# Projections of a conditioned attention layer: block products of 128 output rows, or four products of 32 output rows side by side

## The chip, the cores and the metric

The kernel runs on one core of a Trainium2 chip. The metric is the device time of one execution in microseconds (us), the median of three runs. A core has five engines with a queue of instructions each: TensorE (PE in the profile; its weight loads are listed apart as PEld), VectorE (DVE), ScalarE (ACT), GpSimd (POOL) and SyncE (SP), which here issues nearly all transfers. A matmul of TensorE holds one operand (the stationary one) in the array and streams the other (the moving one) through it; its sums go to PSUM, which has eight banks of 128 partitions x 512 f32.

## The reference

Eight batches of 512 tokens with 512 features go through one attention layer with 16 heads of 32 features; a conditioning token per batch is projected too and added to the queries and keys, and the input is added to the output.

```python
def _L0_cond_ref(x, tokens, Wq, bq, Wk, bk, Wv, bv):
    Q = _split_heads(x @ Wq.T + bq)
    K = _split_heads(x @ Wk.T + bk)
    V = _split_heads(x @ Wv.T + bv)
    tQ = _split_heads(tokens @ Wq.T + bq)
    tK = _split_heads(tokens @ Wk.T + bk)
    cQ = Q + tQ
    cK = K + tK
    scores = jnp.einsum('bhqd,bhkd->bhqk', cQ, cK) / jnp.sqrt(jnp.float32(HEAD_DIM))
    attn = jax.nn.softmax(scores, axis=-1)
    out = jnp.einsum('bhqk,bhkd->bhqd', attn, V)
    ...
x = x + _L0_cond_ref(x, cond_1024[:, None, :], ...)
```

## The kernel before

**Tiling.** Everything is f32 except small bf16 helpers. A *tile of work* t is four heads (128 features) of one batch: T = 8 x 4 = 32 of them, t = 4b + g. Queries and keys stand with features on partitions (`qT`, `kT`, 128 x 512 for one t), values with tokens on partitions (`v`).

**Projections.** The projections Q, K and V are made in 2 x 2 blocks with seven block products in place of eight (`MADE_OF` lists which sum of weight blocks meets which sum of input blocks; `combine_w` and `combine_x` make the sums `wc` and `xc` ahead of time). For one projection n, one batch b and one half u of the output, `product` (L397) makes block product i: a contraction over 256 features in two chunks kc, so two f32 matmuls of a 128 x 128 stationary operand with a 128 x 256 moving one, into half a bank. For q and k the weights are stationary and the input moves (L406); for v the input is stationary and the weights move (L403). `first_products` (L431) makes products 1, 6, half of 2, and 7, with a copy by ACT (`m1`, L438) and three additions by DVE (L444, L445, L429 or L426). `other_products` (L448) makes 4, 5, the other half of 2, and 3, then three wider additions by DVE (L458, L459, L429 or L426). Either one issues seven matmuls. In both, a call `small()` stands in the middle: after product 6, or after product 5.

**Stages.** The order on PE, ACT, DVE and POOL is written out by hand (`manual_schedule`): instructions run on each engine in the order of the code. The main loop (L796, t = 0 to 28) has four stages for each t. Each stage begins with `exponentials` of one 128-token chunk of keys: four matmuls with `onesb` and `maxT` (L560, three rows, bf16) and four with `kT` and `qT` (L563, 32 rows) into four banks, which ACT then takes the exponential of (`e`, L574). Then comes `row_max` of a later chunk: four score matmuls of 32 rows (L499) into the other four banks, from which DVE takes negative row maxima (L490 twice, L508) and after that ACT exponentials with a running sum (`dead`, L518, in `denominators`). Then the stage's own part follows:

- first stage: half of the q products of a later batch (`project_pair`),
- second stage: `weighted` (L617), that is values times `e` in 128 x 32 column tiles (`times_v`, L579), the denominators spread the same way (L610), a transpose by DVE (L635) and the stores,
- third stage: half of the k products,
- fourth stage: half of the v products, with `transpose_max` (L539) as its `small()`: four bf16 128 x 128 transposes on PE (L544) and a copy by DVE (L550) that makes the `maxT` of the next t.

A row of products is made in two stages, `first_products` in one t and `other_products` in the next, so the two alternate. The q and k products in the loop belong to t = 1 to 28, the v products with transposes to t = 0 to 28. Four stages of products stand ahead of the loop (L749 to L761), three of v without transposes in its t = 0 (L806, L822, L832). The last tiles (from L904) have no products.

**PSUM.** All eight banks are one tile; `TURNS` says for each stage which bank is used for what. So a score matmul L499 waits until the bank that it writes has been read: by ACT (`dead` of the stage before) or by DVE (the last addition of the products of the stage before).

**Shapes on TensorE.** Three ways to divide the array occur: 32 rows x 128 columns (L560, L563, L499: four heads side by side on different rows), 128 rows x 32 columns (L579, L610: four outputs side by side on different columns), and the whole 128 x 128 (L403, L406, L544). Every f32 matmul of the code appears in the trace as two weight loads and two matmuls.

Of the kernel before, what the change touches and what calls it, by code (L numbers as in the profile page):

```python
# [17 lines left out]
def kernel(  # L18
# [38 lines left out]
    nc = tc.nc  # L57
    P = 128
    B, S, D = x.shape
    HD = 32  # L60
    H = D // HD
    G = D // P
    HG = P // HD
# [5 lines left out]
    HS = S // 2  # L69
# [175 lines left out]
    for i in range(NS):  # L245
        r = slice(i * BL, (i + 1) * BL)
# [130 lines left out]
    def block_of_w(n, i, u, kc):  # L377
        f = MADE_OF[i - 1][0]
        if n == "v":
            at = slice(0, HS) if f != "22" else slice(HS, D)  # L380
            if isinstance(f, int):
                return wc[n][:, f, kc, :]
        else:
            g = u * 2 + (f == "22")
            at = slice(g * P, (g + 1) * P)
            if isinstance(f, int):
                return wc[n][:, f, kc, u * P : (u + 1) * P]
        return wT[n][:, kc + 2 * (f != "11"), at]

    def block_of_x(b, i, kc, at):  # L390
        f = MADE_OF[i - 1][1]
        if isinstance(f, int):
            return xc[:, f, kc, at]
        off = HS * (f == "22")
        return xT[b][:, kc + 2 * (f != "11"), at.start + off : at.stop + off]

    def product(n, b, u, i, pt, kcs=(0, 1)):  # L397

        for kc in kcs:
            w = block_of_w(n, i, u, kc)  # L400
            if n == "v":
                xb = block_of_x(b, i, kc, slice(u * P, (u + 1) * P))
                nc.tensor.matmul(pt, xb, w, start=(kc == kcs[0]), stop=(kc == kcs[-1]))  # L403
            else:
                xb = block_of_x(b, i, kc, slice(0, HS))
                nc.tensor.matmul(pt, w, xb, start=(kc == kcs[0]), stop=(kc == kcs[-1]))  # L406

    def twice(a):
        return a.unsqueeze(1).broadcast_to([P, 2, HS])
# [21 lines left out]
    def first_products(n, b, u, dens, small, at, first=0):  # L431


        one_, two_ = banks(first), banks(at)
        c1, c12, c2, c22 = parts_of(n, b, u)
        m1 = c2[:, 0, :]
        product(n, b, u, 1, one_[:, :HS])
        nc.scalar.copy(m1, one_[:, :HS])  # L438
        dens()
        product(n, b, u, 6, two_[:, :HS])  # L440
        small()
        product(n, b, u, 2, two_[:, HS:], (0,))
        product(n, b, u, 7, one_[:, HS:])
        nc.vector.tensor_tensor(c12, two_[:, :HS], m1, ALU.add)  # L444
        nc.vector.tensor_tensor(c1[:, 0, :], two_[:, HS:], m1, ALU.add)  # L445
        plus(n, b, u, 1, c22, one_[:, HS:], c12)
# [349 lines left out]
    for t in range(T - 3):  # L796
        b, r = divmod(t, G)
# [201 lines left out]
    b, g = divmod(t, G)  # L999
# [55 lines left out]
```

## Time and profile before

| what | value |
|---|---|
| median of 3 runs (lowest, highest) | 729.93 us (729.53, 730.05) |
| span of the profiled execution, first to last instruction | 727.7 us |
| granted TensorE clock, mean | 1.000 |
| PE busy | 720.6 us (99%), 5412 matmuls |
| PEld busy | 406.0 us (56%), 5412 loads |
| ACT busy | 616.6 us (85%) |
| DVE busy | 536.5 us (74%) |
| POOL busy | 175.9 us (24%) |
| block products of v, L403 | 448 matmul records |
| block products of q and k, L406 | 840 matmul records |

The profiled execution has no time of its own beside its span; the span is 2.2 us below the median of the runs, the part that lies around the first and the last instruction. A group line of the profile gives engine, line, operation, the tiles written and read, and the shape: for a matmul, rows*columns of the stationary operand and then the moving operand. A matmul's record starts when it enters the array; its end is modelled, so records of matmuls that follow each other overlap, and the distance from start to start is what counts. Two numbers at the head of a timeline line are the start in us from the beginning of the span and how long the merged records last; x4 is the number of records; a bracket is idle time of the engine before them and what ended it.

### The profile page before, as it was taken

The numbers are of one execution on the slowest core, as the hardware profiler recorded it, in microseconds if no ns is written. First come the engines' busy times: TensorE is split into PE (matmuls) and PEld (weight loads), VectorE is DVE, ScalarE is ACT, GpSimd is POOL, SyncE is SP. The second block draws the span as 40 slices with busy tenths as digits, with TensorE's granted clock in tenths as the row PEclk, the third lists the DMA queues.
The fourth block names the chain that finished last, engine by engine and source line by source line (L and its number), as shares of the span: only waits on it lengthen the run. The fifth ranks groups of instructions, "written<-read, shape, count | busy, mean of one in ns | idle before, by whom it ended". The sixth has DMA issues, their size and how long they took to land.

```text
span 727.7 us, 15109 instructions
## 1 busy us (share of the span) xinstructions
PE 720.6 (99%) x5412; PEld 406.0 (56%) x5412; DVE 536.5 (74%) x863; ACT 616.6 (85%) x1539; POOL 175.9 (24%) x275
## 2 busy tenths in 40 slices
PE   9999999999999999999999999999999999999997
PEld 7566555566555566555566555565555565555532
DVE  4798777777768777678776877777767777767777
ACT  2589898899898898888899888888988989888664
POOL 3711221122221122221122221122221122221351
PEclk9999999999999999999999999999999999999999
DMA  6743221222221222221222221212110111110111
GB/s 176 110 64 49 45 45 23 38 39 36 44 44 21 40 34 40 45 41 23 42 33 41 44 40 22 44 31 43 31 23 9 31 29 31 30 20 11 30 31 29
DMA packets 207583, 29.12 MB, mean 40 GB/s; under 512 B 205834, under 2 KB 206346, under 8 KB 207508
## 3 DMA queue, kind: packets, MB, share of 16 engines
q1 hardware_dynamic: 205748, 27.11, 22.5%
q10 hardware_dynamic: 1760, 1.05, 0.5%
q8 instruction: 42, 0.69, 0.4%
q14 instruction: 33, 0.27, 0.1%
HBM read 19.75 MB, written 8.39 MB: 39 GB/s over the span
## 4 chain that ended last, share of the span: by engine, by line
PE 96%; DVE 2%; DMA 1%; issue 1%; DVEq 0%; SPq 0%
PE psum L406 27%; PE psum L499 16%; PE psum L579 15%; PE psum L403 14%; PE psum L563 14%; PE psum L560 5%; PE psum L350 2%; PE psum L544 1%; DVE acc L855 1%; DMA x<-in_x_dram 1%; PE psum L881 1%; PE psum L657 0%; DVE acc L853 0%; PE psum L589 0%; PE psum L266 0%
## 5 line engine op out<-in xcount | busy, mean ns | idle before, releaser
L518 ACT ACTIVATE dead<-psum,nmax 128x512 f32<-128x512 f32 x480 | 327.0, 701 | 5.2 <-DVE nmax L490 3.1
L574 ACT ACTIVATE e<-psum 128x512 f32<-128x512 f32 x488 | 251.9, 603 | 71.5 <-PE psum L563 71.2
L490 DVE TENSOR_REDUCE nmax<-psum 128x1 f32<-128x512 f32 x240 | 154.5, 685 | 142.8 <-PE psum L499 142.8
L508 DVE TENSOR_REDUCE nmax<-psum 128x2 f32<-128x1024 f32 x130 | 157.6, 1214 | 2.7 <-PE psum L499 2.7
L499 PE MATMUL psum<-kT,qT 32*128 32x512 f32 x1024 | 142.6, 601 | 0.0
L636 POOL TENSOR_TENSOR res<-res,recs 128x512 f32<-128x512 f32 x30 | 31.4, 1047 | 439.0 <-DVE res L635 439.0
L563 PE MATMUL psum<-qT,kT 32*128 32x512 f32 x976 | 125.5, 587 | 0.0
L579 PE MATMUL psum<-e,v 128*32 128x512 f32 x1024 | 121.2, 597 | 0.0
L518 ACT ACTIVATION_READ_ACCUMULATOR dead<-psum,nmax 128x1 f32 x480 | 104.8, 218 | 0.0
L499 PEld LDWEIGHTS psum<-kT,qT 32*128 32x128 f32 x1024 | 59.7, 183 | 57.1 <-ACT dead L518 19.6
L579 PEld LDWEIGHTS psum<-e,v 128*32 128x32 f32 x1024 | 26.6, 110 | 65.1 <-issue 37.6
L563 PEld LDWEIGHTS psum<-qT,kT 32*128 32x128 f32 x976 | 48.6, 185 | 2.2
L403 PE MATMUL psum<-wc_v,xc 128*128 128x256 f32 x192 | 49.3, 379 | 0.0
L560 PE MATMUL psum<-maxT,onesb 3*128 3x512 bf16 x488 | 48.2, 385 | 0.0
L406 PE MATMUL psum<-xc,wc_k 128*128 128x256 f32 x180 | 46.2, 379 | 0.0
L406 PE MATMUL psum<-xc,wc_q 128*128 128x256 f32 x180 | 46.2, 379 | 0.0
L560 PEld LDWEIGHTS <-onesb 3*128 3x128 bf16 x488 | 12.3, 91 | 57.2 <-issue 47.9
L173 POOL TENSOR_TENSOR xr<-xr,bvs 128x512 f32<-128x512 f32 x31 | 39.3, 1268 | 17.4 <-DMA xr<-in_x_dram 17.4
L403 PEld LDWEIGHTS psum<-wc_v,xc 128*128 128x128 f32 x192 | 36.5, 190 | 4.9
L403 PE MATMUL psum<-wT_v,xT 128*128 128x256 f32 x128 | 38.8, 405 | 0.0
L637 POOL TENSOR_TENSOR res<-res,xr 128x512 f32<-128x512 f32 x30 | 38.2, 1273 | 2.3
L406 PEld LDWEIGHTS psum<-xc,wc_q 128*128 128x128 f32 x180 | 34.2, 190 | 4.6
(165 smaller groups left out, 819.5 us busy)
## 6 DMA issues: line engine op xcount, KB each, us to landing
xr<-in_x_dram SPq DMA_DIRECT2D x124, 64.0 KB, 2.4
out_dram<-res SPq DMA_DIRECT2D x122, 64.0 KB, 1.9
x<-in_x_dram SPq DMA_DIRECT2D x112, 64.0 KB, 2.3
w_q<-in_L_cond_Wq_dram SPq DMA_DIRECT2D x4, 256.0 KB, 4.5
w_v<-in_L_cond_Wv_dram SPq DMA_DIRECT2D x16, 64.0 KB, 2.4
w_k<-in_L_cond_Wk_dram SPq DMA_DIRECT2D x16, 48.0 KB, 2.6
x<-in_x_dram ACTq DMA_DIRECT2D x2, 256.0 KB, 3.9
x<-in_x_dram SPq DMA_DIRECT2D x2, 256.0 KB, 4.1
```

Source lines behind the costliest of these rows:

```text
L173: nc.gpsimd.tensor_tensor(xr[t], xr[t], bias, ALU.add)
L403: nc.tensor.matmul(pt, xb, w, start=(kc == kcs[0]), stop=(kc == kcs[-1]))
L406: nc.tensor.matmul(pt, w, xb, start=(kc == kcs[0]), stop=(kc == kcs[-1]))
L490: nc.vector.tensor_reduce(nmax[t][:, qc, j : j + 1, 0], banks(HG + j), AX.X, ALU.max, negate=True)
L499: nc.tensor.matmul(pt, qkT["q", t][r, qc * P : (qc + 1) * P], qkT["k", t][r, :], start=True, stop=True,)
L508: nc.vector.tensor_reduce(nmax[t][:, qc, pr * 2 : pr * 2 + 2, 0], pt, AX.X, ALU.max, negate=True)
L518: nc.scalar.activation(dead, banks(HG + j), AF.Exp, bias=nmax[t][:, qc, j, :], accum_out=sums[t][:, qc, j, :],)
L560: nc.tensor.matmul(bank[j], onesb[r, :], maxT[t][r, :], start=True, stop=False)
L563: nc.tensor.matmul(bank[j], qkT["k", t][r, kc * P : (kc + 1) * P], qkT["q", t][r, :], start=False, stop=True,)
L574: nc.scalar.activation(e[:, i, :], bank[pr * 2 + i], AF.Exp)
L579: nc.tensor.matmul(pt[j * HD : (j + 1) * HD, :], vs[b % 2][:, kc, (g * HG + j) * HD : (g * HG + j + 1) * HD], es[t, kc, j // 2][:, j % 2, ...
L637: nc.gpsimd.tensor_tensor(y, y, xr.pop(t), ALU.add)
```

## The change

Each matmul of a block product (128 columns of the stationary operand) is written as four matmuls with 32 columns each. Matmul j takes columns 32j to 32j+31 of the stationary operand, streams the same moving operand, and writes partitions 32j to 32j+31 of the output. `start` and `stop` are as before. `HG` is 4 and `HD` is 32. Nothing else of the kernel is changed; `times_v` and `spread_sums` are written in this way already.

```diff
         for kc in kcs:
             w = block_of_w(n, i, u, kc)
             if n == "v":
-                xb = block_of_x(b, i, kc, slice(u * P, (u + 1) * P))
-                nc.tensor.matmul(pt, xb, w, start=(kc == kcs[0]), stop=(kc == kcs[-1]))
+                still, moving = block_of_x(b, i, kc, slice(u * P, (u + 1) * P)), w
             else:
-                xb = block_of_x(b, i, kc, slice(0, HS))
-                nc.tensor.matmul(pt, w, xb, start=(kc == kcs[0]), stop=(kc == kcs[-1]))
+                still, moving = w, block_of_x(b, i, kc, slice(0, HS))
+            for j in range(HG):
+                r = slice(j * HD, (j + 1) * HD)
+                nc.tensor.matmul(
+                    pt[r], still[:, r], moving, start=(kc == kcs[0]), stop=(kc == kcs[-1])
+                )
```

## The prediction, made before the changed kernel ran

> **What bounds the kernel now.** I read the page first (busy time, then the chain that ended last), then TensorE's timeline over some stages, then the timelines of weight loads, VectorE and ScalarE around the stages' borders.
>
> ```profile
> span 727.7 us, 15109 instructions
> ...
> PE 96%; DVE 2%; DMA 1%; issue 1%; DVEq 0%; SPq 0%
> ```
>
> The end is set by PE almost alone. The timeline shows what it pays. First two whole stages (weighted, then one of v), then a place in the tail where four transposes stand between two 128x32 groups:
>
> ```profile
> 313.33 0.40 PE L560 MATMUL psum<-maxT,onesb 3*128 3x512 bf16 x4
> ...
> 314.42 1.02 PE L499 MATMUL psum<-kT,qT 32*128 32x512 f32 x8
> 315.37 1.07 PE L579 MATMUL psum<-e,v 128*32 128x512 f32 x8
> ...
> 316.31 2.76 PE L579 MATMUL psum<-e,v 128*32 128x512 f32 x24
> 319.01 0.40 PE L560 MATMUL psum<-maxT,onesb 3*128 3x512 bf16 x4
> ...
> 325.38 1.11 PE L499 MATMUL psum<-kT,qT 32*128 32x512 f32 x8
> 326.42 1.13 PE L403 MATMUL psum<-wT_v,xc 128*128 128x256 f32 x4
> 327.39 1.03 PE L403 MATMUL psum<-wc_v,xc 128*128 128x256 f32 x4
> 328.25 0.39 PE L544 MATMUL psum<-identb,split 128*128 128x128 bf16 x4
> 328.48 0.65 PE L403 MATMUL psum<-wT_v,xT 128*128 128x256 f32 x2
> 328.96 1.03 PE L403 MATMUL psum<-wc_v,xT 128*128 128x256 f32 x4
> 329.92 0.40 PE L560 MATMUL psum<-maxT,onesb 3*128 3x512 bf16 x4
> ...
> 692.53 1.07 PE L579 MATMUL psum<-e,v 128*32 128x512 f32 x8
> 693.53 0.40 PE L544 MATMUL psum<-identb,split 128*128 128x128 bf16 x4
> 693.86 1.07 PE L579 MATMUL psum<-e,v 128*32 128x512 f32 x8
> ```
>
> Two things are to be seen. The distance from start to start inside one shape is constant: (1.03 - 0.38)/3 = 0.216 us for a 256-column record of L403, (2.76 - 0.59 - 0.02)/5 = 0.429 us for a group of four column tiles of L579, whose four records start 7 ns apart. And every change of shape leaves a hole: the last record of L499 starts at 314.42 + 1.02 - 0.59 = 314.85, streams 0.43, and the next shape starts only at 315.37, 0.09 later; 0.52 from start to start in either stage.
>
> **The streaming.** An f32 matmul of a product is two records of 0.216 us. After the change it is two groups of four records. A group of L579 streams 512 columns in the time that one 128x128 record would take for them (0.429 is twice 0.216 less a few ns), so a group with 256 columns takes 0.216 us as well: 644 product matmuls, 1288 records before, 1288 groups after, difference nothing. No row shows four column tiles reading one moving operand; I allow 1 ns a group either way, 1.3 us.
>
> **Issue.** PE's instructions for a product stage go from 28 to 112 in 14 x 0.216 = 3.02 us, 27 ns each. The trace bounds this from both sides. The highest rate that it holds over microseconds is the weighted stage: 40 loads and 40 matmuls (L579 and 8 of L610) from 315.37 to 319.01, 46 ns each; were that the most that TensorE is fed, a stage would last 112 x 46 = 5.15 us, +2.1, and 92 stages +196 us. In a burst right after a wait the eight loads at 325.32 (below) start within 0.34 - 0.18 = 0.16 us with seven matmuls between them, 15 instructions at 11 ns. The weighted stage is paced by its streams (0.429 a group), not by its feed, so the burst is the nearer row, and I cost issue at nothing; the streaming hides it.
>
> **Weight loads.** The record of a load falls from 190 ns (128 columns) to 110 (32 columns). Loads hide beneath the matmul before them, so only the first after a hole shows: the first L403 group lasts 1.13 where an unhindered one lasts 1.03, so 0.104 us (483 against 379 ns for its first record). The first record of L579 lasts 617 against a median of 592 ns, so 0.025 us. Each product stage gains 0.079 us on entry. What if the cover is gone and every group shows its load: 1288 x 0.025 = 32 us. L579's loads start 2 ns after the matmul before and leave its 0.429 unchanged, so I take nothing.
>
> The Trainium skill (TensorE: Matmul & The Clock Gate, "What overlaps and what doesn't") speaks against the change here: it says that a weight load runs beside a matmul only if the two use different row groups, and column tiles all use the same rows. With its load time (columns / 1.2 ns, so 27 ns) that would be an estimated 1288 x 27 ns = 35 us. The same page ("Wait — 56ns, not 53.3ns?") gives 62 ns of sequencer time for a matmul when hardware decoding is off; 56 matmuls a stage would be 3.5 us for 3.02, an estimate of up to 41 us over 92 stages. The start of L579's loads contradicts the one, the burst the other.
>
> **Leaving a product stage.** Before: last record of L403 at 328.96 + 1.03 - 0.38 = 329.61, L560 at 329.92, 0.31. From column tiles: last L579 record at 316.31 + 2.76 - 0.59 = 318.48, L560 at 319.01, 0.53, less 0.213 for the shorter stream, 0.31 again; but the last tile starts 0.02 after the first. Cost 0.020 us a stage. Entry and exit together: -0.059 us.
>
> **The transposes in the v stages** are where a cost is added. Before, L544 has the same shape as L403 and no hole. Afterwards it stands between column tiles, and the tail shows just this. There, from the last tile of the group ahead (692.53 + 1.07 - 0.59 = 693.01) to the last tile of the second group behind (694.34) is 1.33 us; two streams of 256 columns fewer give 1.33 - 2 x 0.213 = 0.90. Before, 328.04 to 328.75 is 0.71. Cost 0.19 us, two holes in place of none. So a v stage with transposes pays -0.059 + 0.188 = +0.129 us.
>
> **PE alone** would give: 92 product stages, of them 29 of v with transposes (+0.129), 62 plain (-0.059), and one ahead of the loop that has its transposes in front (148 against 55 ns to the first product, 241 against 273 ns to the second group, 20 ns on leaving: +0.081). Sum 3.74 - 3.66 + 0.08 = +0.16 us.
>
> **But the gains of q and k meet another wait.** What is next late is the bank for the scores L499 in the stage behind:
>
> ```profile
> 321.15 1.29 DVE L490 TENSOR_REDUCE nmax<-psum 128x1 f32<-128x512 f32 x2 [1.20 <-PE psum L499]
> 324.45 0.75 DVE L429 SCALAR_TENSOR_TENSOR kT<-psum,tok,kT 128x512 f32<-128x512 f32 x1
> ...
> 298.45 2.06 ACT L574 ACTIVATE e<-psum 128x512 f32<-128x512 f32 x4 [0.95 <-PE psum L563]
> 303.21 0.24 ACT L518 ACTIVATION_READ_ACCUMULATOR dead<-psum,nmax 128x1 f32 x1
> ...
> 325.32 0.34 PEld L499 LDWEIGHTS psum<-kT,qT 32*128 32x128 f32 x8 [0.60 <-ACT dead L518]
> 303.51 0.30 PEld L499 LDWEIGHTS psum<-kT,qT 32*128 32x128 f32 x6 [0.23 <-ACT dead L518]
> ```
>
> Behind `other_products`, VectorE runs without a pause from L490 (freed by the scores of the same stage) through L508, L458, L459 to L429, which ends at 325.20; the loads of L499 start at 325.32, and its group lasts 1.11 where an unhindered one lasts 1.02: 0.09 us lost. Behind `first_products`, ScalarE runs without a pause from `e` (freed by L563) over the copy and four `dead` to 303.45; the load comes at 303.51 and the scores lose 0.09 again. Both chains begin ahead of the products, so neither moves when the products end 0.059 sooner: L499 ends when it did. The q `other` kind, 0 to 14 ns from its wait in the trace (load 314.30, exposed 0.10, matmul 314.42), has nothing to give either. So the 56 loop stages of q and k give nothing, bounds -3.3 us (all of it, if no chain held) and +1 us (20 ns a stage if loads bunch). In the v stages no such cover helps: the scores of the q stage behind them (L499 at 309.15, lasting 1.02) wait for nothing, so the cost is whole.
>
> **Sum.** 29 x 0.129 = +3.74 us; four stages ahead of the loop, 3 x -0.059 + 0.081 = -0.10; three v stages of t = 0, two of them held, -0.06 at most; the edge of q, 14 x -0.003 = -0.04. Total +3.6 us: span 727.7 to 731.3, and with the 2.2 us between span and median, 729.93 to **733.5 us** (0.5% slower).
>
> **Rivals.**
>
> *A, the gains are kept* (VectorE and ScalarE are let go earlier too): then PE's own sum, +0.16 us, 730.1. For it: 96% of the chain is PE. Against: the two waits above. 13%.
>
> *B, loads or issue show.* In column tiles of 256 columns the load has half the cover that it has in L579. If each group shows 25 ns, 32 us: 762. It decides once a load takes over 0.216 us in all; its record is 110 ns. 6%.
>
> *C, faster: the holes beside the transposes don't open*, because whole-array transposes follow column tile by column tile. Then v stages gain 0.059 too and, with A's gains, 92 x -0.059 = -5.4 us, 724.5; with q and k held 728.2. It decides if L544 starts within 0.25 us of the last product group ahead. Against: 693.01 to 693.53 in the tail, of which 0.09 is hole. 5%.
>
> *D, the four tiles don't run side by side*: 1288 x 3 x 0.216 = +835 us. L579 says no; 1%.
>
> **Chances and range.** The forecast, 732 to 735.5 by 1 ns a group and 20 ns a stage, has 68%; mixed cases between A and it, 4%, further small costs above it, 3%. A measurement of this kernel tells some 0.2% (1.5 us) from no change. Faster by more is C, 0.05; within, A and half of the mixed cases, 0.15; slower, the rest, 0.80. The range reaches down to A and up to 737: 729.9 to 737.
>
> **What would show it.** L406 and L403 as 128*32 in 5152 records of each kind, groups 0.216 us apart, the first record of a stage some 25 ns longer; L499's last record to the first product still 0.52; L560 0.31 behind the last tile; L544 about 0.31 behind the last tile of the product ahead and the next product 0.15 behind its last; v stages of 5.63 us at 5.76, q and k stages followed by a later L499, with its wait on `dead` and L429 grown by 0.06. A group pitch over 0.22, L544 without holes, or shorter pairs of q and k with the stage behind would prove me wrong.

## The result, and the profile after

The changed kernel takes 732.1 us (731.91 to 732.62, six runs) where the kernel before, on the same chip, takes 729.75 us (729.47 to 730.35): a ratio of 1.0033, 95% interval 1.0021 to 1.0044, so 2.4 us slower. The span of the profiled execution goes from 727.7 to 730.4 us, +2.7. Line numbers behind the change are 3 higher: L560 is L563, L563 is L566, L499 is L502, L518 is L521, L429 is L432, L544 is L547, and all products are L407.

The page of the changed kernel, first the busy times, then the chain:

```profile
span 730.4 us, 22837 instructions
...
PE 723.7 (99%) x9276; PEld 325.6 (45%) x9276; DVE 537.4 (74%) x863; ACT 617.9 (85%) x1539; POOL 176.8 (24%) x275
...
PE 97%; DVE 2%; issue 1%; DVEq 0%
```

PE sets the end as before, and it has 3864 matmuls more. PEld is less busy (45% for 56%): four loads of 32 columns run side by side in 110 ns each, where one of 128 took 190. The timeline of PE over one v stage of the changed kernel (start us, us, line, tiles, shape, records), the same stage as the one shown of before:

```profile
326.31 1.14 PE L502 MATMUL psum<-kT,qT 32*128 32x512 f32 x8
327.38 1.07 PE L407 MATMUL psum<-wT_v,xc 128*32 128x256 f32 x16
328.27 1.05 PE L407 MATMUL psum<-wc_v,xc 128*32 128x256 f32 x16
329.25 0.40 PE L547 MATMUL psum<-identb,split 128*128 128x128 bf16 x4
329.58 0.64 PE L407 MATMUL psum<-wT_v,xT 128*32 128x256 f32 x8
330.03 1.05 PE L407 MATMUL psum<-wc_v,xT 128*32 128x256 f32 x16
331.01 0.39 PE L563 MATMUL psum<-maxT,onesb 3*128 3x512 bf16 x4
```

Sixteen records of L407 last 1.05 us where four whole ones lasted 1.03: the four tiles run side by side, 0.216 us a group. The first sixteen last 1.07 where the first four lasted 1.13: that is the shorter first load. But the transposes start at 329.25, and the last product ahead of them began at 328.27 + 1.05 - 0.38 = 328.94; 0.31 from start to start where the stream is 0.21, so 0.09 us of hole, and another one behind them (329.25 to 329.58, where the transposes were followed after 0.23). And the scores L502 last 1.14 where they lasted 1.11: they wait longer.

Read from the trace, the median lengths of the stages in us, from one L560/L563 to the next, with what the scores L499/L502 lose in them to a late bank (their last start behind 1.526 us) in brackets:

| stage | before | after |
|---|---|---|
| q and k (half of the k stages with `other_products` 0.02 longer before, 0.01 after) | 5.265 (0) | 5.205 (0) |
| weighted, behind `first_products` of q | 5.775 (0.095) | 5.841 (0.161) |
| weighted, behind `other_products` of q | 5.679 (0) | 5.704 (0.024) |
| v, behind `first_products` of k | 5.633 (0.089) | 5.827 (0.154) |
| v, behind `other_products` of k | 5.630 (0.085) | 5.787 (0.115) |

Without the brackets a v stage goes from 5.544 to 5.673: +0.129 us.

### The profile page after: what moved, and what is told of

The parts are those of the page before. It is cut to its first block, busy times and chain, and to the rows that moved or that the text cites. A ratio compares the mean times of both kernels' runs of the same rounds, so it can differ in the third digit from the quotient of the medians.

```text
span 730.4 us, 22837 instructions
## 1 busy us (share of the span) xinstructions
PE 723.7 (99%) x9276; PEld 325.6 (45%) x9276; DVE 537.4 (74%) x863; ACT 617.9 (85%) x1539; POOL 176.8 (24%) x275
## 3 DMA queue, kind: packets, MB, share of 16 engines
q10 hardware_dynamic: 1760, 1.05, 0.5%
## 4 chain that ended last, share of the span: by engine, by line
PE 97%; DVE 2%; issue 1%; DVEq 0%
PE psum L407 40%; PE psum L502 16%; PE psum L582 15%; PE psum L566 14%; PE psum L563 5%; PE psum L350 2%; PE psum L547 1%; DVE acc L858 1%; PE psum L884 1%; PE psum L682 0%; PE psum L266 0%; DVE acc L856 0%; PE psum L311 0%; PE psum L660 0%; PE psum L592 0%
## 5 line engine op out<-in xcount | busy, mean ns | idle before, releaser
L521 ACT ACTIVATE dead<-psum,nmax 128x512 f32<-128x512 f32 x480 | 328.1, 707 | 5.5 <-DVE nmax L493 3.1
L502 PE MATMUL psum<-kT,qT 32*128 32x512 f32 x1024 | 145.2, 604 | 0.0
L566 PE MATMUL psum<-qT,kT 32*128 32x512 f32 x976 | 125.5, 587 | 0.0
L521 ACT ACTIVATION_READ_ACCUMULATOR dead<-psum,nmax 128x1 f32 x480 | 107.3, 224 | 0.0
L502 PEld LDWEIGHTS psum<-kT,qT 32*128 32x128 f32 x1024 | 59.6, 183 | 60.1 <-ACT dead L521 20.2
L407 PE MATMUL psum<-wc_v,xc 128*32 128x256 f32 x768 | 50.2, 379 | 0.0
L566 PEld LDWEIGHTS psum<-qT,kT 32*128 32x128 f32 x976 | 48.6, 185 | 2.2
L563 PE MATMUL psum<-maxT,onesb 3*128 3x512 bf16 x488 | 48.1, 385 | 0.0
L407 PE MATMUL psum<-xc,wc_q 128*32 128x256 f32 x720 | 47.1, 379 | 0.0
L407 PE MATMUL psum<-xc,wc_k 128*32 128x256 f32 x720 | 47.1, 379 | 0.0
L563 PEld LDWEIGHTS <-onesb 3*128 3x128 bf16 x488 | 12.3, 91 | 64.3 <-issue 52.8
L407 PE MATMUL psum<-wT_v,xT 128*32 128x256 f32 x512 | 37.5, 387 | 0.0
L407 PE MATMUL psum<-xT,wT_k 128*32 128x256 f32 x480 | 34.5, 382 | 0.0
L407 PE MATMUL psum<-xT,wT_q 128*32 128x256 f32 x480 | 34.5, 382 | 0.0
```

Source lines behind the costliest of these rows:

```text
L407: nc.tensor.matmul(pt[r], still[:, r], moving, start=(kc == kcs[0]), stop=(kc == kcs[-1]))
L502: nc.tensor.matmul(pt, qkT["q", t][r, qc * P : (qc + 1) * P], qkT["k", t][r, :], start=True, stop=True,)
L521: nc.scalar.activation(dead, banks(HG + j), AF.Exp, bias=nmax[t][:, qc, j, :], accum_out=sums[t][:, qc, j, :],)
L563: nc.tensor.matmul(bank[j], onesb[r, :], maxT[t][r, :], start=True, stop=False)
L566: nc.tensor.matmul(bank[j], qkT["k", t][r, kc * P : (kc + 1) * P], qkT["q", t][r, :], start=False, stop=True,)
```

## The experiments

Theory H is the one that was predicted: two holes around the transposes of the v stages cost, and what q and k gain is taken back by the banks that ScalarE (`dead`) and VectorE (the last addition) give back too late. As the expectations state it, H has one thing already from the trace of the changed kernel: behind `other_products` only about half of the gain is taken back. Rival A: PE alone decides. Rival B: column tiles cost something in every product stage. Differences in us are against the kernel before on the same chip.

**1 and 10. Column tiles for q and k alone** (C is 128 for v), run twice:

```diff
-            for j in range(HG):
-                r = slice(j * HD, (j + 1) * HD)
+            C = P if n == "v" else HD
+            for j in range(P // C):
+                r = slice(j * C, (j + 1) * C)
```

> Only the products of q and k are done in column tiles; v stays in whole-array matmuls. Theory H (the cost lies in the two holes around the transposes of the v stages, and what q and k gain is mostly held by ScalarE's dead and VectorE's last addition): q and k stages 60 ns shorter, the stage behind first_products 60 to 66 ns longer, the stage behind other_products some 25 to 30 ns longer; 28 x -0.033 us kept, -0.1 ahead of the loop, so about -0.9 us against before (bounds -0.4 to -1.4), 728.8. Rival A (PE alone decides): 60 stages x -0.059 = -3.5 us, 726.3. Rival B (column tiles cost something in every product stage, 2.4 us over 92 stages): +1.6 us, 731.3.

> The products of q and k alone in column tiles once more, as the first time scattered from 728.9 to 731.0. H2: q and k stages 60 ns shorter, taken back whole behind first_products and by half behind other_products: -0.6 to -0.9 us against before. PE alone: -3.5 us.

Measured: 729.71 against 729.42 (ratio 1.0003, interval 0.9994 to 1.0012), then 729.9 against 729.41 (1.0006, 0.9997 to 1.0015). The executions scatter from 728.9 to 731.0, those of before from 729.05 to 729.92. The profiled one was the fastest both times (728.9; span 727.1, -0.6), and in it the stages are as H has them: q and k 5.205, the weighted stage behind `first_products` 5.842 and 5.836, v behind k 5.70 and 5.66. Rival A (726.3) is out, and B's 731.3 lies above both intervals. The median misses H's -0.6 to -0.9 as well: that q and k keep a part of their gain is seen in the traces, not in the medians of this kernel. What lengthens its other executions by up to 2 us was not found.

**2. Column tiles for v alone** (C is 32 for v, 128 else):

> Only the products of v are done in column tiles; q and k stay whole. H: 29 v stages +0.129 us each, 5.63 to 5.76 us, q and k stages and the stages behind them as before: +3.6 us against before (bounds +3.2 to +3.9), 733.4, more than the whole change costs. Rival B: 32/92 of 2.4 us, +0.8 us, 730.6.

Measured: 733.44 against 729.42, ratio 1.0054 (1.0042 to 1.0067), +4.0, just above the bounds; the spans differ by 3.7. v stages last 5.768 and 5.758. A part of the change (32 of 92 product stages) costs more than all of it: B falls, and the cost sits in the v stages.

**3. The transposes in column tiles too.** If the change of shape is what costs, it can be taken away:

```diff
-            nc.tensor.transpose(
-                pt[:, qc * P : (qc + 1) * P],
-                split[t % 2][:, qc, :, :].rearrange("p h e -> p (h e)"),
-                identb,
-            )
+            for h in range(HG):
+                nc.tensor.transpose(
+                    pt[h * HD : (h + 1) * HD, qc * P : (qc + 1) * P],
+                    split[t % 2][:, qc, h, :],
+                    identb,
+                )
```

> The change as it is, and the transposes of maxT too are done in column tiles (four of 32 rows of output side by side in place of one of 128), so that no shape changes inside a v stage. H: no holes of 0.09 us around L544, and the 57 ns that the first load behind the transposes cost before are gone too; v stages 0.116 us shorter than before, half of them held again in the q stage behind by VectorE's last addition; with the 0.9 us of q and k about -3.2 us against before (bounds -2.0 to -4.5), 726.5. Rival B: as slow as the change, +2.4 us, 732.1.

Measured: **724.93** against 729.42, ratio 0.9939 (0.9926 to 0.9951), -4.5: faster than either kernel. PE's timeline of this kernel:

```profile
324.94 1.05 PE L407 MATMUL psum<-wc_v,xc 128*32 128x256 f32 x16
325.80 0.41 PE L548 MATMUL psum<-identb,split 128*32 128x128 bf16 x16
326.03 0.61 PE L407 MATMUL psum<-wT_v,xT 128*32 128x256 f32 x8
326.46 1.05 PE L407 MATMUL psum<-wc_v,xT 128*32 128x256 f32 x16
```

From the last product tile (324.94 + 1.05 - 0.38 = 325.61) to the first transpose is 0.19 in place of 0.31, from the transposes' start to the next product 0.23 in place of 0.33, and the next eight records last 0.61: no hole, no exposed load. At -4.5 the gain is at the end of the bounds. Half of the q stages behind v, those with `first_products`, lose 0.083 to VectorE as expected; what was not reckoned is that this is not lost again behind them: the weighted stage that follows lasts 5.790, not 5.841. The loop itself is 3.7 us shorter than before. Another 0.8 us came ahead of its first stage (45.60 before, 45.43 in the changed kernel, 44.84 here); as this start lies anywhere from 45.1 to 46.0 us in the other traces, it isn't shown how much of that is due to the edit.

**4. Two tiles of 64 columns** (C is 64 throughout):

> All products in two column tiles of 64 in place of four of 32. H: the first load shows about half of the 104 ns (some 53, so 51 ns gained on entry), the holes around the transposes are the same; v stages +0.16 us, q and k 44 ns shorter and mostly held: about +4.0 us against before (bounds +3.0 to +4.7), 733.7, more than with 32. Rival B (a cost for each tile): half of the change's cost or less, +1.2 us, 730.9.

Measured: 733.31 against 729.42, ratio 1.0052 (1.0039 to 1.0064), +3.9. The two orders of the theories are opposite, and H's is seen: fewer tiles cost more. Against the change with four tiles the order is clear in the stages (q and k 5.218 for 5.205, v 5.841 and 5.802 for 5.827 and 5.787), less so in the times, whose intervals overlap. PE's timeline:

```profile
327.51 1.08 PE L408 MATMUL psum<-wT_v,xc 128*64 128x256 f32 x8
328.43 1.03 PE L408 MATMUL psum<-wc_v,xc 128*64 128x256 f32 x8
329.39 0.40 PE L548 MATMUL psum<-identb,split 128*128 128x128 bf16 x4
329.72 0.65 PE L408 MATMUL psum<-wT_v,xT 128*64 128x256 f32 x4
```

The first group shows 0.05 us of load, half of the 0.10 of 128 columns; the holes around the transposes are the same.

**7. The converse: products whole, transposes alone in column tiles** (the edit of experiment 3 in the kernel before):

> The kernel before, products whole, and only the transposes of maxT in column tiles: the same mismatch of shapes inside the v stages the other way round. H: holes of 0.09 us on both sides of the transposes again, and the first product load behind them shows its 104 ns: from the last product record ahead to the second behind 0.98 us in place of 0.71, 29 x 0.27 = +7.7 us against before (bounds +6.5 to +8.5), 737.2. Rival B (the products in column tiles cost, the transposes don't): +0.2 us or less, 729.6.

Measured: 736.78 against 729.43, ratio 1.0100 (1.0086 to 1.0114), +7.4. PE's timeline:

```profile
330.30 1.03 PE L403 MATMUL psum<-wc_v,xc 128*128 128x256 f32 x4
331.26 0.41 PE L545 MATMUL psum<-identb,split 128*32 128x128 bf16 x16
331.59 0.70 PE L403 MATMUL psum<-wT_v,xT 128*128 128x256 f32 x2
```

With the products as they were, 0.31 from the last of them (330.95) to the transposes, and two records that last 0.70 where they lasted 0.65. It is the mismatch that costs, whichever side of it is tiled.

**5 and 6. The holders made shorter.** Maxima and `dead` exponentials over 384 of 512 keys, in the kernel before and in the changed one (the maxima and denominators then leave out a quarter of the keys):

```diff
+    NW = 384
...
-                    nmax[t][:, qc, j : j + 1, 0], banks(HG + j), AX.X, ALU.max, negate=True
+                    nmax[t][:, qc, j : j + 1, 0], banks(HG + j)[:, :NW], AX.X, ALU.max, negate=True
...
-            nmax[t][:, qc, pr * 2 : pr * 2 + 2, 0], pt, AX.X, ALU.max, negate=True
+            nmax[t][:, qc, pr * 2 : pr * 2 + 2, 0], pt[:, :, :NW], AX.X, ALU.max, negate=True
...
-                dead,
-                banks(HG + j),
+                dead[:, :NW],
+                banks(HG + j)[:, :NW],
```

> The kernel before with the maxima (VectorE) and the dead exponentials (ScalarE) over 384 of 512 keys in place of all: both chains that hold the scores are some 0.4 us shorter a stage, and PE's work is the same. The softmax denominators and shifts are of 384 keys. H: the 86 to 97 ns that the scores lose in three of eight stages, and the 20 in one, go away: about -3.9 us against before (bounds -3 to -6, the ends of the program get shorter too), 725.5. If the scores were held by something else: no change.

> The changed kernel with the same 384 keys. H: nothing holds what q and k gain, so against the kernel of the run before this one it is PE's own sum: 29 x 0.129 - 62 x 0.059 + 0.08 = +0.2 us (bounds -0.3 to +0.7). Rival B (a cost of column tiles in every product stage), and any other holder of the gains: the +2.4 to +2.7 us of the change.

Measured: 726.74 against 729.43 (0.9960, 0.9946 to 0.9974), -2.7 where -3 to -6 was expected, and 727.46 (0.9972, 0.9961 to 0.9984): +0.7 between them, not +0.2. One half of H holds: behind `first_products` nothing is lost any more (weighted 5.680, v 5.544). The edit shortens VectorE's work too, but there VectorE had long been done in the kernel before (L429 ends at 302.54 + 0.48 = 303.02, the scores are loaded at 303.51), so ScalarE was the holder. The other half fails: v behind `other_products` of k still lasts 5.630 and loses 0.085, though VectorE's work ahead is 0.5 us shorter. VectorE's timeline of experiment 5 shows why:

```profile
278.99 0.68 DVE L460 TENSOR_TENSOR kT<-psum,kT 128x512 f32<-128x512 f32 x1
279.93 0.75 DVE L430 SCALAR_TENSOR_TENSOR kT<-psum,tok,kT 128x512 f32<-128x512 f32 x1 [0.26 <-PE psum L407]
```

and the timeline of the weight loads of the scores behind it:

```profile
280.80 0.34 PEld L500 LDWEIGHTS psum<-kT,qT 32*128 32x128 f32 x8 [0.60 <-issue]
```

The last addition (L430 here, L429 before) now stands idle for 0.26 us until the product L407 is done, and ends at the same distance from it: 279.93 + 0.75 = 280.68, the loads at 280.80. So theory H2: behind `other_products` the scores wait for the last product's own signal and the addition behind it.

**8 and 9. The last addition in two halves**, so that only a shorter one stands behind the last product:

```diff
-        plus(n, b, u, 0, c1, halves(two_), c1)
+        for i in range(2):
+            plus(n, b, u, 0, c1[:, i, :], two_[:, i * HS : (i + 1) * HS], c1[:, i, :])
```

> The kernel before with 384 keys in the maxima and the dead exponentials, and the last addition of other_products done in two halves, the first of which needs product 2 alone. H2 (what holds the scores behind other_products is no chain of VectorE's own but the signal of the last product and the addition of 0.75 us behind it): the addition behind the last product falls to some 0.48 us, the 84 ns that 14 v stages still lose go away: -1.2 us against the narrow kernel with the whole addition (726.7), so 725.5. If VectorE's chain held them: no change or later, as its work grows by 0.2 us a stage.

> The changed kernel with the same two edits (384 keys, the last addition in halves). H2: nothing holds the scores any more in either kernel, so against the run before this one it is PE's own sum, 29 x 0.129 - 62 x 0.059 + 0.08 = +0.2 us (bounds -0.3 to +0.6). If something else takes back what q and k gain: +0.7 to +1.0 us, as between the narrow kernels with the whole addition.

Measured: 730.45 and 731.67, 1.2 us apart and not 0.2. The edit did the opposite of what was meant. VectorE's timeline of experiment 8:

```profile
280.66 0.88 DVE L430 SCALAR_TENSOR_TENSOR kT<-psum,tok,kT 128x256 f32<-128x256 f32 x2 [0.27 <-PE psum L407]
```

Both halves wait for the last product, and together they last 0.88 us in place of 0.75. The suspected cost is 0.13 us larger, then, and the stages behind `other_products` grow by just that: v from 5.630 to 5.770, weighted from 5.680 to 5.813. 28 stages by 0.13 is 3.7 us; measured 730.45 - 726.74 = 3.7. VectorE had 0.27 us to spare ahead of the addition, so its own chain can't have been the holder.

**11 and 12. Only half of the last addition**, with the 384 keys (the other half of `c1` then lacks a block product):

```diff
-        plus(n, b, u, 0, c1, halves(two_), c1)
+        plus(n, b, u, 0, c1[:, 1, :], two_[:, HS:], c1[:, 1, :])
```

> The kernel before with 384 keys in the maxima and the dead exponentials, and of the last addition of other_products only the half that needs product 3 (256 of 512 columns; the other half of c1 lacks a block). Nothing is added anywhere. H2 (the scores behind other_products wait for the signal of the last product and the addition behind it): the addition falls from 0.75 to some 0.48 us, the 84 ns that 14 v stages lose go away, -1.2 us against the narrow kernel with the whole addition (726.7): 725.5. If something else holds those stages: 726.7.

> The changed kernel with the same edits. H2: no scores are held in either kernel, and the change costs PE's own sum, +0.2 us against the run before this one (bounds -0.3 to +0.6). If the gains of q and k are taken back by something else still: +0.7 to +1.2 us.

Measured: 725.11 (0.9942, 0.9929 to 0.9954) and 725.24 (0.9944, 0.9931 to 0.9958). All v stages with transposes last 5.544 and 5.671, weighted ones 5.679 in both, q and k 5.265 and 5.205: nothing is held any more, and the change costs +0.13 us, PE's own sum (the loop alone is 0.17 us longer in the trace). Between the whole kernels it costs 2.4. The difference is what the two holders keep.

## Why the prediction came out as it did

**The direction and the cause are right.** +3.6 us was forecast, +2.4 measured (+2.7 between the profiled spans), at the lower end of the forecast. Step by step:

*Streaming, issue, loads.* No cost, as said: groups 0.216 us apart, 22837 instructions for 15109. All four tiles use the same rows, and the group of 0.216 us stays 0.216 with loads of 110 ns beneath it; four matmuls in 0.216 us are 54 ns each. The Trainium skill (TensorE: Matmul & The Clock Gate, "What overlaps and what doesn't") lets a weight load run beside a matmul only on different row groups, and this trace does not agree. The 62 ns a matmul that the same page gives ("Wait — 56ns, not 53.3ns?") hold for hardware decoding switched off; no run here shows how it is set, and the 54 ns lie below them.

*Entry and exit.* -0.059 forecast, -0.060 measured in the median q and k stage. 64 columns gave 5.218, between the two.

*The transposes.* +0.129 forecast from one place in the tail, +0.129 measured, in 29 stages. Experiments 2, 3, 4 and 7 put it on the change of shape. The size is 0.09 us for each change, plus the first load: 0.025, 0.05 or 0.10 us for 32, 64 or 128 columns. The Trainium skill (TensorEngine Tiling (Array Packing), "Key Properties") says that a change of tiling mode drains TensorE, without a size.

*ScalarE behind `first_products`.* Forecast that it takes the gain back whole; it does (0.060 gained, 0.065 lost), and experiment 5 takes the holder away. ScalarE's last record of `dead` in the changed kernel, and the loads of the scores behind it, in the stage of which the prediction shows 303.21 and 303.51 before:

```profile
304.10 0.26 ACT L521 ACTIVATION_READ_ACCUMULATOR dead<-psum,nmax 128x1 f32 x1
```

```profile
304.36 0.35 PEld L502 LDWEIGHTS psum<-kT,qT 32*128 32x128 f32 x6 [0.23 <-issue]
```

The loads start where ScalarE ends, at 304.10 + 0.26 = 304.36 (before: 303.51 behind 303.45).

*VectorE behind `other_products`: the step that failed.* The prediction said "VectorE runs without a pause from L490 [...] to L429", and that this chain begins ahead of the products, so that "neither moves when the products end 0.059 sooner". The chain does pause. VectorE's timeline shows the last addition and the record ahead of it, first before and then after:

```profile
323.82 0.68 DVE L459 TENSOR_TENSOR kT<-psum,kT 128x512 f32<-128x512 f32 x1
324.45 0.75 DVE L429 SCALAR_TENSOR_TENSOR kT<-psum,tok,kT 128x512 f32<-128x512 f32 x1
```

```profile
324.82 0.68 DVE L462 TENSOR_TENSOR kT<-psum,kT 128x512 f32<-128x512 f32 x1
325.42 0.75 DVE L432 SCALAR_TENSOR_TENSOR kT<-psum,tok,kT 128x512 f32<-128x512 f32 x1
```

From start to start it is 0.63 us before and 0.60 after. Before, L429 waits for the last product of its own stage, just long enough that the record ahead of it hides the wait in the timeline. The queue's own line in the trace of before has it:

```profile
L429 DVEq EVENT_SEMAPHORE  x60: 21/396/648, 32.3 to 674.2; - x60
```

(a count, then least, median and most ns of a wait; behind `other_products` it is 0.45 us). So the holder moves with the product: before and after, and in experiments 5 and 6 too, the addition ends 0.83 us after the product's signal. By the trace's semaphores, a whole product raises its signal 393 ns after the start of its last record, one in four column tiles 422 ns after the start of its last tile, one of two tiles 403. The last tile starts 0.059 us sooner than the last whole record did, the signal comes 0.029 later after it, and 0.03 us is left: the weighted stage loses 0.025 of the 0.060, v 0.030 more than before. Experiments 5 and 6, where VectorE has 0.26 us to spare, lose the same (weighted 0 and 0.024, v 0.085 and 0.116), so the product's signal sets it. In the changed kernel VectorE's own chain has no pause left (L432 overlaps the record ahead by 324.82 + 0.68 - 325.42 = 0.08 us, as L459 overlaps L458 before), so a larger gain would have met that chain. 28 stages keep some 0.033 us each, -0.9 us where the term was put at 0. That is the forecast's excess: 3.6 - 0.9 = 2.7, the span's difference (the 2.4 of the medians has an interval of 1.5 to 3.2). The smaller terms, 0.005 a stage lost behind `first_products` (+0.15 in all), 0.1 us more gained ahead of the loop and in its first round, and 0.1 in k stages, roughly cancel; the second of them is within what the start of the loop scatters by from trace to trace.

*Rivals.* A's number, +0.16, is right for a kernel without the two holders (+0.13 in experiments 11 and 12) and wrong for this one. B, C and D did not come: loads hidden, holes open, tiles side by side.

## What to carry to other kernels

Column tiles are worth their shorter first load only where they add no change of shape. The q and k stages, with row tiles on both sides of the products before and after, gain 0.06 us; the v stages, with whole transposes in between, lose 0.13. Count the changes of shape, 0.09 us each here, before and after, and tile the small matmuls in between as well. An engine that is 99% busy still gives a gain back at once if the buffer it needs next is freed by a chain that starts elsewhere; follow each gain to the next wait, and ask of every chain that seems unbroken whether one of its links waits for the very work that moves. Looking at a queue's semaphore waits, and not only at idle gaps between records, answers it.

## What was not expected of the hardware

The signal of a product in four column tiles comes 29 ns later after the start of its last tile than that of a whole one (10 ns with two tiles), on top of the 20 ns by which the last tile starts behind the first. The Trainium skill (TensorE: Matmul & The Clock Gate, "The cost: per-tile semaphore tail") has a tail that grows by 4.7 ns a tile, an estimated 14 ns for four tiles against one. Counted from the start of the last tile, the traces show twice that.

Two executions of one kernel can differ more than two kernels do: column tiles in q and k alone scattered over 2 us, the changed kernel over 0.7.
